# Inverse deviations of all norms by GpSimd's power, and a new hand-over between blocks, in a four-layer hybrid network

## The chip, the core and the metric

The kernel runs on one core of a Trainium2 chip. The core has a matrix engine (TensorE, PE in the profile; its weight loads are shown apart as PEld), a vector engine (VectorE, DVE), an engine for activation functions (ScalarE, ACT), a general engine (GpSimd, POOL) and an engine that in this kernel only issues transfers (SyncE, SP). Each works through its own instructions in order and waits at semaphores for the others. The metric is the device time of one launch in microseconds (us): the median of several runs. One execution is profiled, and every duration below is from it.

## What is computed

The input is four images of 128 channels and 64 x 64 pixels in float32. Four layers follow each other, each with a residual sum and a norm ahead of it:

```python
# layers 0 and 1: norms over groups of 4 channels (_gn)
x = x + L0_conv(_gn(x), ...)      # depthwise convolutions, sorting of patches, a state-space scan
x = x + L1_conv(_gn(x), ...)      # 3x3 convolution
t = _to_tokens(x)                 # 4096 tokens of 128 channels an image
t = t + L2_attn(_ln_t(t), ...)    # attention, 16 heads of 8, then a small feed-forward part
t = t + L2_ffn(_ln_t(t), ...)     # 64 experts, each picks its 8 best tokens
t = t + L3_attn(_ln_t(t), ...)    # linear attention
t = t + L3_ffn(_ln_t(t), ...)     # 64 experts again

def _ln_t(v, eps=1e-5):
    m = jnp.mean(v, axis=-1, keepdims=True)
    s = jnp.var(v, axis=-1, keepdims=True)
    return (v - m) / jnp.sqrt(s + eps)
```

Inside layer 2's attention, with t already normed:

```python
attn_out = ctx @ w_comb.T + b_comb
x1 = _ln(x + attn_out, g1, beta1)           # x is the normed input
zf = jnp.cos(x1[..., :8]) * jnp.cos(ry_theta)
h = jax.nn.relu(zf @ w1.T + b1)
return _ln(x1 + h @ w2.T + b2, g2, beta2)
```

What matters here is the factor 1/sqrt(s + 1e-5), which every norm needs once a token (or once a channel in `_gn`).

## The kernel before

Tokens or pixels lie along the free dimension, 128 channels on the partitions, and the 4096 columns of an image are worked through in 8 chunks of 512 (`NCH`, `CH`). Four stretches follow each other in time.

**Layers 0 and 1** (`layers01`, lines 270 to 1074). The first image is brought into sorted order alone (`in_order`); then `scan` runs over all four images, 8 chunks each, while the preparation of the next image, or the convolution of a finished one, runs beside it. In the scan the order of the instructions of all five engines is the written one (`tc.manual_schedule`). Small steps are put off with `later` and issued at the next `flush`, which stands between the decays (L908, ScalarE) and the scans (L912, VectorE) of every half step; GpSimd multiplies the states at L916. The groupnorm (`groupnorm_scale`) takes its root at L204 and inverts it at L200; the pixel norm takes its roots for four chunks together at L654, inverts at L659, and spreads them with transposes at L668.

**Layer 2** (`layer2_attention`). For each image b, a stage with planned order runs `prepare(b)` (norm, cosines, products, stores of the heads) beside `feed_forward(b - 1)` (what follows the attention of the image before); then `attention` of image b runs, with the written order on TensorE, VectorE and GpSimd. Outside the parts in `manual_schedule`, the framework's planner orders the instructions by the time at which it thinks them ready, and by the order of the program among the ready ones. `run` takes a step of each of its parts in turn. `feed_forward` is a chain of nine stages a chunk: `fetch` (den, num, nrm_in), `divisors`, `attended`, `first_centred`, `first_norm`, `cosines`, `hidden`, `last_centred`, `last_norm`; so there are two norms a chunk in it, and one in `prepare`. The first 1024 columns of an image (its chunks 0 and 1) get a further sum, from `around_d`: `attention` stores for each head h the sums `accs[h][:, 0]` as one [128, 256] block (L1437), and `gathered` reads them for a chunk with 16 transfers, one a head (L1583). `divisors` turns den's 2 x 16 rows to columns with a matmul against `pick`, which adds the two halves.

**The shared norm** (`layernorm_steps`, L99 to L126). TensorE subtracts the mean (`ln_xc`); ScalarE squares (L107) and copies (L109); TensorE takes the mean of the squares (`ln_var`); VectorE transposes 32 x 32 blocks (L115), so that four variances lie in columns; ScalarE takes the root (L117), VectorE inverts it (L118), TensorE spreads the four columns with transposes against the identity (L121), and VectorE multiplies (L123, or L125 with a GpSimd addition at L126). `first_centred` gives it two terms: `w_comb` times the attended sums and `center` times nrm_in.

**The experts** (`expert_ffn`, twice) **and layer 3** (`layer3_attention`, between them). `weigh` goes through 16 steps a pair of images: `centred`, `deviation` (a transpose of 64 x 512 at L1782, the root at L1784, the inverse at L1785, a transpose back at L1786) and `gates`. The second pair's steps run beside `collect` of the first. Layer 3 runs `summed(b + 1)`, with the shared norm in it (L1973), beside `answered(b)`; image 0's `summed` runs alone.

In the profile, ScalarE has besides its activations instructions named ACT_TABLE_LOAD, which stand ahead of an activation whose function needs another table than the one in place.

Of the kernel before, what the change touches and what calls it, by code (L numbers as in the profile page):

```python
# [30 lines left out]
class Common:  # L31
# [3 lines left out]
    def __init__(self, tc, pool):  # L35
# [18 lines left out]
        self.eps5 = const("eps5", [P, 1], 1e-5)  # L54
# [44 lines left out]
    def layernorm_steps(self, out, terms, work, psum, affine=None, bufs=2):  # L99
# [7 lines left out]
        nc.scalar.activation(sq, xc, AF.Square, bias=shift)  # L107
        kept = work.tile([P, CH], F32, name="ln_kept", bufs=bufs)
        nc.scalar.activation(kept, xc, AF.Identity, bias=shift)  # L109
# [6 lines left out]
        sd = work.tile([P, 4, 1], F32, name="ln_sd")  # L116
        nc.scalar.activation(sd, vt[:, :, 0:1], AF.Sqrt, bias=self.eps5)  # L117
        nc.vector.reciprocal(sd, sd)  # L118
        by_block = vp.rearrange("p (g b i) -> p b g i", b=4, i=32)
        for k in range(4):  # L120
            nc.tensor.transpose(by_block[:, k], sd[:, k].to_broadcast([P, P]), self.ident)  # L121
        if affine is None:
            nc.vector.tensor_tensor(out, kept, vp, ALU.mult)  # L123
        else:
            nc.vector.scalar_tensor_tensor(kept, kept, g, vp, ALU.mult, ALU.mult)  # L125
            nc.gpsimd.tensor_scalar(out, kept, b, None, ALU.add)  # L126

# [35 lines left out]
    def groupnorm_scale(self, xb, xp, small, psum):  # L163
# [33 lines left out]
        sd = small.tile([P, 1], F32, name="gn_sd")  # L197

        def offset():
            nc.vector.reciprocal(rs, sd)  # L200
            nc.vector.scalar_tensor_tensor(off, gm, -1.0, rs, ALU.mult, ALU.mult)

        def deviation():
            nc.scalar.activation(sd, vp, AF.Sqrt, bias=self.eps5)  # L204
            self.later(offset)
# [64 lines left out]
def layers01(K, xd, dpool, w, w1):  # L270
# [9 lines left out]
    with ExitStack() as ctx:  # L280
# [145 lines left out]
        def in_order(b, made, work, psum):  # L426
# [208 lines left out]
            spreads = small.tile([P, NCH, 4], F32, name="spreads")  # L635
# [3 lines left out]
            def varied(c):  # L639
# [12 lines left out]
                def root():  # L652
                    at = spreads[:, c - 3 : c + 1]
                    nc.scalar.activation(at.unsqueeze(3), kept["vt"][:, :, :, 0:1], AF.Sqrt, bias=K.eps5)  # L654
                    later(inverted)

                def inverted():
                    at = spreads[:, c - 3 : c + 1]
                    nc.vector.reciprocal(at, at)  # L659
# [4 lines left out]
            def scaled_by_root(n):  # L664
                bp = K.bank(psum, [P, CH], "pos_rs")
                by_block = bp.rearrange("p (g b i) -> p b g i", b=4, i=32)
                for k in range(4):
                    nc.tensor.transpose(by_block[:, k], spreads[:, n, k : k + 1].to_broadcast([P, P]), K.ident)  # L668
# [436 lines left out]
def layer2_attention(K, xd, dpool, w):  # L1105
# [6 lines left out]
    with ExitStack() as ctx:  # L1112
# [48 lines left out]
        pick = cst.tile([2 * NH, NH], F32, name="pick")  # L1161
        nc.vector.tensor_tensor(pick, K.ident[0 : 2 * NH, 0:NH], K.ident[0 : 2 * NH, NH : 2 * NH], ALU.add)
# [22 lines left out]
        around_d = dpool.tile([NH, P, L // NJ // 4], F32, name="around_d")  # L1185
# [135 lines left out]
        def attention(qt, first, dsum, big, two, work, pssc, psctx, psacc):  # L1321
# [83 lines left out]
            def turn():  # L1405
# [28 lines left out]
                if i == 0:  # L1434


                    nc.sync.dma_start(out=around_d[h], in_=accs[h][:, 0].rearrange("p t r -> p (t r)"))  # L1437
# [121 lines left out]
        def feed_forward(b, dsum, work, psum):  # L1559
# [17 lines left out]
            def gathered(c):  # L1577
# [4 lines left out]
                for h in range(NH):  # L1582
                    nc.sync.dma_start(  # L1583
                        out=part[HD * h : HD * h + HD],
                        in_=around_d[h, :, c * P : (c + 1) * P].rearrange("(n d) f -> d n f", d=HD),
                    )
                    if h % 4 == 3:
                        yield
                yield
# [8 lines left out]
            def firsts():  # L1598
                for c in order[NCH - CHB :]:
                    yield from gathered(c)  # L1600

            def divisors(c):
                num, den, at = loads[c]
                tp = psum.tile([P, 4, NH], F32, name="den_t", tag="mm")
                for j in range(4):
                    mm(tp[:, j, :], den[:, j * P : (j + 1) * P], pick)
                rd = work.tile([P, 4, NH], F32, name="rd")
                nc.vector.tensor_tensor(rd, tp, dsum[:, 4 * c : 4 * c + 4], ALU.add)
# [13 lines left out]
            def first_centred(c):  # L1622
# [3 lines left out]
                    x1, [(w_comb, num[:, 0]), (K.center, nrm)], work, psum, (b_comb, g1, beta1), bufs=3  # L1626
# [47 lines left out]
        for b in range(NB + 1):  # L1674
            with (
# [3 lines left out]
                with (  # L1679
# [3 lines left out]
                    parts = list(feed_forward(b - 1, past, work, psum)) if b > 0 else []  # L1683
                    if b < NB:
                        part, qt, first = prepare(b, big, two, work, psum)
                        parts.append(part)
                    run(*parts)
# [15 lines left out]
def expert_ffn(K, xs, w, tag):  # L1703
# [10 lines left out]
    with ExitStack() as ctx:  # L1714
# [47 lines left out]
        def weigh(pr):  # L1762
# [3 lines left out]
            sqs = {}  # L1766
# [367 lines left out]
```

## Time and profile before

| What | us |
|---|---|
| median of 3 runs (9885.13 to 9886.97) | 9885.43 |
| the profiled execution, its own time | 9881.09 |
| its span, first to last instruction | 9879.3 |
| busy: PE / DVE / ACT / POOL | 8736.1 / 7220.5 / 7410.6 / 4802.8 |
| mean granted TensorE clock | 0.92 |

The stretches in time, read from the windows of the profile (us from the start of the span):

| Stretch | from | to | length |
|---|---|---|---|
| first image brought in order | 0 | 190 | 190 |
| scan, with the work beside it | 190 | 2645 | 2455 |
| last convolution | 2645 | 2745 | 100 |
| first `prepare`, alone | 2745 | 2880 | 135 |
| four attentions | | | 1291, 1291, 1293, 1290 |
| three stages with `feed_forward` and `prepare` | 4171 | 4371 | 200 each |
| last `feed_forward`, alone | 8627 | 8765 | 138 |
| experts of layer 2 | 8765 | 9130 | 365 |
| layer 3 | 9130 | 9520 | 390 |
| experts of layer 3 | 9520 | 9880 | 360 |

A line of the list of groups reads: line of the kernel, engine, operation, written tile <- read tiles, shapes, count | busy time in all, mean ns of one | idle time of the engine just before, and what ended it. A line of the timeline gives start, length, engine, line, operation and, in brackets, the idle time before it and its releaser. A line of the windows gives the stretch, its length, the busy time of PE, PEld, DVE, ACT and POOL with their instructions, the granted clock, the share of the transfer engines and GB/s.

### The profile page before, as it was taken

Reading aid. Unit: us, or ns where it says so; the run is one execution under the profiler, and the core shown is the slowest. Engines: PE = TensorE matmul, PEld = TensorE weight load, DVE = VectorE, ACT = ScalarE, POOL = GpSimd, SP = SyncE. Lnnn points to the kernel's source line nnn. Section 1 sums busy time; section 2 is a strip of 40 time slices with the busy share of each in tenths; the row PEclk is TensorE's granted clock in tenths of the full one; section 3 lists DMA queues with packets and bytes.
Section 4 is the critical chain, followed back from the end, with each engine's and each line's share of the span. In section 5 each row is a group of like instructions: output and inputs, shape, how many; then the busy total and the mean of one; then the engine's idle time right before and its main releaser. Section 6 shows DMA issues by size and latency. Waiting matters only on the chain.

```text
span 9879.3 us, 187787 instructions
## 1 busy us (share of the span) xinstructions
PE 8736.1 (88%) x74074; PEld 3348.6 (34%) x74074; DVE 7220.5 (73%) x7877; ACT 7410.6 (75%) x10669; POOL 4802.8 (49%) x3175
## 2 busy tenths in 40 slices
PE   5888888888869999989999989999989999967776
PEld 2222222244523333333333333333333333333433
DVE  2889897988658888758888758888758888743463
ACT  3766767654359999879999879999879999841531
POOL 1677676765435555455555455555455555420000
PEclk8887878889979999989999989999989999988997
DMA  4524435223121221231111131211131211124004
GB/s 116 124 69 118 97 83 125 67 76 88 46 70 40 40 40 41 48 94 39 40 39 41 46 97 39 40 40 39 44 101 39 39 40 39 40 93 121 1 18 154
DMA packets 575731, 635.31 MB, mean 64 GB/s; under 512 B 113080, under 2 KB 369152, under 8 KB 573824
## 3 DMA queue, kind: packets, MB, share of 16 engines
q1 hardware_dynamic: 574848, 623.30, 25.6%
q8 instruction: 584, 9.57, 0.4%
q14 instruction: 299, 2.45, 0.1%
HBM read 446.84 MB, written 109.07 MB: 56 GB/s over the span
## 4 chain that ended last, share of the span: by engine, by line
PE 69%; DVE 10%; POOL 6%; ACT 5%; DMA 4%; issue 3%; SPq 2%; DVEq 0%; POOLq 0%; ACTq 0%
PE ctx_ps L91 27%; PE acc_ps L91 13%; PE score L91 11%; PE conv L91 4%; DVE hs L912 3%; POOL hs L916 3%; PE ln_xc L91 2%; PE y_ps L91 2%; DVE hs L901 2%; PE xc_ps L91 1%; DMA w<-in_L_ffn_weight 1%; PE ln_var L91 1%; PE b_ps L91 1%; PE hid_ps L91 1%; PE kv L91 1%
## 5 line engine op out<-in xcount | busy, mean ns | idle before, releaser
L1535 ACT ACTIVATE ex<-score 128x1024 f32<-128x1024 f32 x5120 | 4925.4, 1036 | 218.5 <-PE score L91 125.7
L91 PE MATMUL ctx_ps<-ex,qt 128*32 128x512 f32 x20480 | 2733.9, 606 | 19.9 <-DVE ctx L1469 19.9
L1484 POOL TENSOR_TENSOR folded<-ex 128x1024 f32<-128x1024 f32 x512 | 1224.2, 2391 | 2101.5 <-ACT ex L1535 1836.6
L1541 DVE STREAM_TRANSPOSE turned<-ex 128x1024 f32<-128x1024 f32 x1536 | 1885.8, 1228 | 329.1 <-ACT ex L1535 328.7
L1517 DVE STREAM_TRANSPOSE turned<-ex 128x1024 f32<-128x1024 f32 x1532 | 1842.4, 1203 | 0.0
L91 PE MATMUL acc_ps<-turned,turned_v 128*32 128x256 f32 x24576 | 1769.5, 379 | 3.1 <-POOL qt L1229 2.3
L912 DVE TENSOR_TENSOR_SCAN hs<-decay,carry,hs 128x512 f32<-128x512 f32 x1024 | 1245.7, 1266 | 193.6 <-ACT decay L908 180.1
L91 PE MATMUL score<-queries,keys 32*128 32x512 f32 x10240 | 1335.3, 497 | 44.0 <-POOL queries L1219 37.9
L91 PEld LDWEIGHTS acc_ps<-turned,turned_v 128*32 128x32 f32 x24576 | 800.9, 110 | 1476.5 <-issue 1323.8
L916 POOL TENSOR_TENSOR hs<-hs,c_sb 128x1024 f32<-128x1024 f32 x512 | 1207.3, 2358 | 81.4 <-DMA c_sb<-c_d 40.3
L908 ACT ACTIVATE decay<-dt,a_neg 128x512 f32<-128x512 f32 x1024 | 693.0, 689 | 662.5 <-DVE hs L912 653.3
L91 PEld LDWEIGHTS score<-queries,keys 32*128 32x128 f32 x10240 | 512.6, 182 | 1139.2 <-ACT ex L1535 780.9
L1347 POOL TENSOR_TENSOR turned_v<-v,quarter 128x1024 f32<-128x1024 f32 x256 | 612.4, 2393 | 265.7 <-PE acc_ps L91 225.0
L91 PE MATMUL y_ps<-hs,pair 128*64 128x512 f32 x2048 | 661.5, 773 | 33.6 <-POOL hs L916 33.6
L1485 POOL TENSOR_TENSOR quarters<-folded 128x512 f32<-128x512 f32 x512 | 657.7, 1285 | 40.2
L91 PEld LDWEIGHTS ctx_ps<-ex,qt 128*32 128x32 f32 x20480 | 406.4, 108 | 654.7 <-issue 598.7
L901 DVE TENSOR_TENSOR hs<-dtx,b_ps 128x2048 f32<-128x2048 f32 x256 | 580.1, 2266 | 55.9 <-PE b_ps L91 31.6
L91 PE MATMUL b_ps<-dbc,state 32*64 32x512 f32 x1024 | 343.2, 752 | 233.4 <-DVE hs L901 233.2
L1535 ACT ACTIVATION_READ_ACCUMULATOR ex<-score 128x1 f32 x2048 | 435.9, 213 | 0.0
L915 POOL COPY carry<-hs 128x2 f32<-128x2 f32 x512 | 98.1, 192 | 673.4 <-DVE hs L912 652.0
L1469 DVE COPY ctx<-ctx_ps 128x512 f32<-128x512 f32 x256 | 176.9, 691 | 329.3 <-PE ctx_ps L91 327.0
L1526 DVE TENSOR_REDUCE dacc<-quarters 128x2 f32<-128x512 f32 x508 | 327.1, 644 | 0.0
(371 smaller groups left out, 9016.1 us busy)
## 6 DMA issues: line engine op xcount, KB each, us to landing
c_sb<-c_d SPq DMA_DIRECT2D x512, 128.0 KB
queries<-head_d SPq DMA_DIRECT2D x1024, 64.0 KB
keys<-head_d SPq DMA_DIRECT2D x1024, 64.0 KB
under<-image_d SPq DMA_DIRECT2D x192, 264.0 KB
dt<-dt SPq DMA_DIRECT2D x128, 256.0 KB
dtx<-dtx SPq DMA_DIRECT2D x128, 256.0 KB
v<-value_d SPq DMA_DIRECT2D x1024, 32.0 KB
w<-in_L_ffn_weight SPq DMA_DIRECT2D x32, 1024.0 KB
```

The costliest lines, as they stand in the source:

```text
L91: self.nc.tensor.matmul(out, lhsT, rhs, start=start, stop=stop)
L901: nc.vector.tensor_tensor(hs, dtx2, bb.unsqueeze(1).to_broadcast([P, NQ, CH]), ALU.mult)
L908: nc.scalar.activation(ex, dt2[:, q, :], AF.Exp, scale=a_neg[:, q, g : g + 1])
L912: nc.vector.tensor_tensor_scan(hs[:, q, :], decays[q - 2 * i], hs[:, q, :], carry[:, g, q : q + 1], ALU.mult, ALU.add)
L916: nc.gpsimd.tensor_tensor(hs[:, two, :], hs[:, two, :], cs.unsqueeze(1).to_broadcast([P, 2, CH]), ALU.mult)
L1347: nc.gpsimd.tensor_tensor(t, v.unsqueeze(2).to_broadcast([P, 4 * BT, 4, HD]), quarter.unsqueeze(1).to_broadcast([P, 4 * BT, 4, HD]), ALU.mult,
L1484: nc.gpsimd.tensor_tensor(hs, exs[:, :, 0], exs[:, :, 1], ALU.add)
L1485: nc.gpsimd.tensor_tensor(qs, hs[:, :, 0 : CH // 2], hs[:, :, CH // 2 :], ALU.add)
L1517: nc.vector.transpose(*upright)
L1526: nc.vector.tensor_reduce(at, qs, AX.X, ALU.add)
L1535: nc.scalar.activation(ex, sps[p], AF.Exp, scale=scale, accum_out=sums[:, t : t + 1] if summed else None)
L1541: nc.vector.transpose(*upright)
```

## The change

Roots: ScalarE's Sqrt and VectorE's reciprocal give way to an addition of 1e-5 on VectorE and a power of -0.5 on GpSimd, everywhere.

```diff
-        sd = work.tile([P, 4, 1], F32, name="ln_sd")
-        nc.scalar.activation(sd, vt[:, :, 0:1], AF.Sqrt, bias=self.eps5)
-        nc.vector.reciprocal(sd, sd)
+        sd = work.tile([P, 4], F32, name="ln_sd")
+        self.inverse_root(sd, vt[:, :, 0])()
...
+    def inverse_root(self, out, src):
+        p, n = out.shape
+        self.nc.vector.tensor_scalar(out, src, 1e-5, None, ALU.add)
+        return lambda: self.nc.gpsimd.tensor_tensor(out, out, self.minus_half[0:p, 0:n], ALU.pow)
...
         def offset():
-            nc.vector.reciprocal(rs, sd)
             nc.vector.scalar_tensor_tensor(off, gm, -1.0, rs, ALU.mult, ALU.mult)
         def deviation():
-            nc.scalar.activation(sd, vp, AF.Sqrt, bias=self.eps5)
+            self.inverse_root(rs, vp)()
             self.later(offset)
```

In the pixel norm the addition is issued at one flush and the power, with `roots[0]`, at the next (`root`, `inverted`). In the expert gates the transpose back becomes a stage of its own, so that it comes one step after the power:

```diff
-                sd = work.tile([P, CH // 32, 1], F32, name="ln_sd")
-                nc.scalar.activation(sd[half], vt[half, :, 0:1], AF.Sqrt, bias=K.eps5[half])
-                nc.vector.reciprocal(sd[half], sd[half])
+                sd = sds[n] = work.tile([P, CH // 32], F32, name="ln_sd")
+                nc.vector.tensor_scalar(sd[half], vt[half, :, 0], 1e-5, None, ALU.add)
+                nc.gpsimd.tensor_tensor(sd[half], sd[half], K.minus_half[half], ALU.pow)
+
+            def spreaded(n):
...
-            return in_turn(2 * NCH, centred, deviation, gates)
+            return in_turn(2 * NCH, centred, deviation, spreaded, gates)
```

The first block's sums: the layout of `around_d` is turned, each head but the last stores 16 pieces of 8 rows, the last head stores one block of its own, and a chunk is read with two transfers.

```diff
+                    sums = accs[h][:, 0].rearrange("p t r -> p (t r)")
+                    if h + 1 < NH:
+                        for k in range(16):
+                            r = slice(HD * k, HD * k + HD)
+                            nc.sync.dma_start(out=around_d[k, HD * h : HD * h + HD], in_=sums[r])
+                    else:
+                        nc.sync.dma_start(out=around_last_d, in_=sums)
...
-                for h in range(NH):
-                    nc.sync.dma_start(
-                        out=part[HD * h : HD * h + HD],
-                        in_=around_d[h, :, c * P : (c + 1) * P].rearrange("(n d) f -> d n f", d=HD),
-                    )
-                    if h % 4 == 3:
-                        yield
-                yield
+                cols = slice(c * P, (c + 1) * P)
+                r = HD * (NH - 1)
+                nc.sync.dma_start(out=part[0:r], in_=around_d[:, 0:r, cols].rearrange("n q f -> q n f"))
+                nc.sync.dma_start(out=part[r:], in_=around_last_d[:, cols].rearrange("(n d) f -> d n f", d=HD))
+                yield from [None] * 4
...
             def firsts():
+                yield from [None] * 12
```

The divisors and the first inner norm: den is turned with transposes, and its halves are added on VectorE; nrm_in is added on VectorE (argument `more`) and no longer goes through `center`, and ScalarE's copy falls away there.

```diff
-                    mm(tp[:, j, :], den[:, j * P : (j + 1) * P], pick)
+                    nc.tensor.transpose(tp[:, j, :], den[:, j * P : (j + 1) * P], K.ident[0 : 2 * NH, 0 : 2 * NH])
                 rd = work.tile([P, 4, NH], F32, name="rd")
-                nc.vector.tensor_tensor(rd, tp, dsum[:, 4 * c : 4 * c + 4], ALU.add)
+                nc.vector.tensor_reduce(rd, tp.rearrange("p j (z h) -> p j h z", z=2), AX.X, ALU.add)
+                nc.vector.tensor_tensor(rd, rd, dsum[:, 4 * c : 4 * c + 4], ALU.add)
...
-                    x1, [(w_comb, num[:, 0]), (K.center, nrm)], work, psum, (b_comb, g1, beta1), bufs=3
+                    x1, [(w_comb, num[:, 0])], work, psum, (b_comb, g1, beta1), bufs=3, more=nrm
...
+        if more is not None:
+            nc.vector.scalar_tensor_tensor(kept, xc, shift, more, ALU.add, ALU.add)
+            nc.scalar.activation(sq, kept, AF.Square)
```

The hand-over: `prepare`'s steps stand ahead of `feed_forward`'s in each turn.

```diff
-                    parts = list(feed_forward(b - 1, past, work, psum)) if b > 0 else []
+                    parts = []
                     if b < NB:
                         part, qt, first = prepare(b, big, two, work, psum)
                         parts.append(part)
+                    if b > 0:
+                        parts.extend(feed_forward(b - 1, past, work, psum))
```

## The prediction

> **What bounds the kernel now.** I read the page's busy row and its table loads first, then the stages by windows, then the order of time inside the stages that the change touches. ScalarE's table loads in the list of groups (count, busy time, mean ns):
>
> ```profile
> L117 ACT ACT_TABLE_LOAD x93 | 119.3, 1283 | 3.8 <-DVE ln_vt L115 2.2
> ...
> L241 ACT ACT_TABLE_LOAD x58 | 74.4, 1283 | 1.0
> ...
> L2023 ACT ACT_TABLE_LOAD x24 | 30.8, 1283 | 0.4
> ...
> L204 ACT ACT_TABLE_LOAD x8 | 10.3, 1283 | 0.1
> L1992 ACT ACT_TABLE_LOAD x8 | 10.3, 1283 | 0.1
> ```
>
> L117 and L204 (with L654, 7 loads, and L1784, 3) are square roots of norms; L241 (Sin) and L2023/L1992 (Exp) mostly load back what a square root drove out. No Square, Identity, Relu or Copy line has a load in these stages, so without the roots one table stays for a whole stage. The stages, by windows (length; then busy time of PE, weight loads, DVE, ACT, POOL; granted clock):
>
> ```profile
> 190.00:2645.00 2455.00, 2042.21 (x7253) 735.36 (x7252) 2085.76 (x1734) 1536.85 (x2056) 1667.62 (x1263) 0.84 0.37 92
> 2745.00:2880.00 135.00, 44.17 (x178) 22.68 (x178) 58.71 (x144) 50.88 (x74) 41.60 (x69) 0.56 0.37 98
> 2880.00:4171.00 1291.00, 1283.04 (x14592) 453.03 (x14592) 1036.39 (x1055) 1237.23 (x1792) 679.23 (x353) 1.00 0.19 38
> 4171.00:4371.00 200.00, 145.43 (x666) 73.73 (x666) 95.33 (x219) 127.84 (x193) 96.28 (x112) 0.80 0.46 128
> 9220.00:9520.00 300.00, 237.64 (x976) 127.20 (x970) 188.87 (x386) 166.35 (x255) 0.58 (x2) 0.99 0.02 6
> ```
>
> The four attention blocks (third row, 1291 us each) are full of TensorE work, 1283 of 1291; the change leaves that work alone. The scan (first row) is paced by VectorE. The rest, a first preparation (135 us), three handovers from block to block (200 each), a last feed-forward (138) and layer 3 (390), has no full engine: there latency decides. In layer 3's steady loop, one chunk takes 10.24 us:
>
> ```profile
> 9240.32 1.28 ACT L117 ACT_TABLE_LOAD   x1
> 9240.70 0.31 DVE L115 STREAM_TRANSPOSE ln_vt<-ln_var 128x128 f32<-128x128 f32 x1
> ...
> 9241.41 1.02 PE L91 MATMUL o_ps<-vn,wo 128*128 128x512 f32 x2
> 9241.62 0.30 ACT L117 ACTIVATE ln_sd<-ln_vt,eps 128x4 f32<-128x4 f32 x1
> ...
> 9242.47 0.75 DVE L2047 SCALAR_TENSOR_TENSOR x<-o_ps,bo,x 128x512 f32<-128x512 f32 x1 [1.46 <-PE o_ps L91]
> 9242.51 1.28 ACT L2023 ACT_TABLE_LOAD   x1
> 9243.14 0.17 DVE L118 RECIPROCAL ln_sd<-ln_sd 128x4 f32<-128x4 f32 x1
> ...
> 9243.36 0.65 PE L121 MATMUL ln_var<-ident,ln_sd 128*128 128x128 f32 x4 [0.93 <-DVE ln_sd L118]
> ```
>
> The root comes so late that the reciprocal (L118) falls behind L2047 on VectorE, and TensorE stands 0.93 us before L121, although its o_ps work ended at 9242.43.
>
> **The price of the power.** No row raises to a power. Its cheapest neighbours on GpSimd are the 128x2 copy at L915 (0.19 us) and the 128x64 product at L1269 (0.31). From above I bound it by GpSimd's dearest elementwise pass, 2.39 us for 128x1024 (L1484): a power of 4 columns would then cost as much as 256 products a column. It is nearest to the small rows but does more per element: I take 0.5 us for 4 columns and 1.0 for 16, ends 0.19 and 2.4. The addition of 1e-5 on VectorE stands in for the reciprocal (0.17 and 0.25 us) and costs no more. A root today, where it needs its load, takes 1.28 + 0.30 + 0.17 = 1.75 us.
>
> The Trainium skill's "GPSIMD Engine Reference", section 3.1, speaks against the edit: elementwise work there costs about twice VectorE's time, and a freshly loaded kernel's first call pays about 6 us. The first half agrees with this trace (1.27 us at L1667 against 0.69 at L123, both 128x512); no row here shows the second. By the page the sum below would be some 6 us higher.
>
> **Part by part.** (a) Layer 3, 24 steady chunks: L115 ends at 9241.01, the addition at about 9241.1, the power at 9241.6, before o_ps ends (9242.43). L121 then starts 0.93 earlier, of which I count 0.85: -20 us. At 2.4 us a power ends at 9243.5, 0.2 after today's reciprocal: +5.
>
> (b) Its first 8 chunks, alone, 11.41 us each: the Exp load (9142.71 to 9144.00) holds up ln_sq behind it, 1.2 us; then ln_vt ends at 9146.07, and the power at 9146.7 stands against the reciprocal at 9147.52, 0.9. Seven periods x 2.1 = -15; at the dear end -1.
>
> (c) The first preparation, 10.95 us a chunk: ln_vt is ready at 2791.21, but the root's load waits for Abs on ScalarE and L118 ends at 2793.36. With the power at 2791.8 and Sin without its load, 2 us x 7 = -14; dear end 0.
>
> (d) The last feed-forward: TensorE is nearly full there (110 of 138). Removed per chunk: the centring product of nrm_in (1.02 us, 8699.09) and half of den_t's eight passes (1.06 us, 8701.02; four transposes are left), 1.55 x 8 = -12; its starting gathers hold den's second load at SP from 8630.43 to 8637.18, -6. Sum -18.
>
> (e) Three handovers. TensorE's waits there: "PE ln_var L121 <- DVE ln_sd L118: 26.6, 13" and "PE ln_xc L91 <- DMA x_in<-xd: 8.0, 1". Of the 26.6 I give back half (13), since the power now queues behind GpSimd passes of 1.3 to 2.4 us. x_in, today issued at 4175.18 behind eight other transfers and landing in 7.74, goes first and may land in the 3.97 of the first preparation (2751.77): 3.6 + 3.8, so -7. Of the 12.4 us of removed matmul work (8 x 1.55) some 5 lies bare, TensorE being busy 145 of 200. Together -25 each, -75; dear end -10 each.
>
> (f) The scan and the start: 16 roots in groupnorms and pixel norms, 12 of them in the scan. Six powers of groupnorms in the scan queue behind products of 2.35 us on GpSimd, and VectorE's gn_off waits: the flush for gn_off comes one slot later (289.37), and the power could end at 287.9 or, behind the other product, at 290.2: 0 to 1 us each, +3. Given back: 12 loads and their returns on ScalarE, busy 63% there, whose lateness costs VectorE 180 us in all; 30 us of 1537 would be 3.5. Zero, with the start -4 (three roots there, little beside them: 1.28 + 0.3 less each).
>
> (g) The expert gates: transposes of root n move one stage later. Two steps take 5.69 us (8821.94 to 8827.63), TensorE busy 42 of 50; the power of 16 columns must fit in one step, 2.84, and one more stage of depth eats what the shorter wait gives: 0.
>
> (h) The sums: fifteen heads x 16 stores of 8 rows in place of one. A store of the same form (num_d, L1474) takes SP 0.30 us from issue to issue, so 16 x 0.30 - 0.34 = 4.5 us a head. SP's waits in a block (343 on ctx, 154 on turned_v, 98 on acc) sum to over half of its 1291 us, so this hides; behind it stand loads of v for GpSimd, two steps ahead. Bare, it would cost 4.5 x 15 x 4 = 270. The fetch shrinks from 16 issues to 2 a chunk and is counted in (d) and (e).
>
> The Trainium skill's "DMA: Bandwidth & Descriptors", rules for kernel authors, says that transfers under 64 KB pay mostly overhead and should be joined. That speaks against (h)'s 8 KB stores; the SP rows show the 16 KB num_d stores hidden behind waits. By its fixed 2 us each, one after another, a block would have 240 x 2 = 480 us more of transfers.
>
> VectorE takes over the sum with nrm (0.75 us, by L125) and a reduction of den (0.25, by L1608), eight times a handover: 95 + 8 = 103 of some 175, hidden.
>
> Sum: -20 - 15 - 14 - 18 - 75 - 4 = -146 against the profiled run's 9881.1 (span 9879.3), giving 9735; the median of the runs, 9885.4, stands 4.3 above it, so 9740. The dear ends give +5 - 1 + 0 - 18 - 30 = -44, so 9841. Cheap ends: in each handover all of 26.6 + 8 + 12.4 (141 for three), 1.3 a chunk in (a) (31), (b) 15, 2.6 a chunk in (c) (18), 24 in (d), 4 in (f): -233, so 9650.
>
> **The rivals.** *GpSimd becomes the queue in the handovers.* It is busy 96 of 200, 24 powers make it 108, and it serves in order: a power behind L126 (1.56) and L1667 (1.27), themselves waiting for VectorE, arrives as late as the root did. For it: "POOL x L126 <- DVE ln_kept L125: 11.6" shows it standing at its head. Against: the root stands behind four hid activations (2.4 us) in the same way. Then only x_in and the matmuls count there, -12 each, and (c) and (d) halve: -36 - 20 - 15 - 7 - 9 - 4 = -91, so 9795.
>
> *The power is dear per element, and the expert gates become its queue.* If it costs 0.6 us a column (2.4 for 4, 9.6 for 16), 32 steps in the bare gates of 2.84 us and 32 beside the collection (67 us for 16, 4.2) grow to 9.6: 216 + 173 = 389 us, against -44 of the rest: 10230. It decides from about 0.33 us a column, where 5.2 us a step costs 75 + 32 = 107 and the rest gives about as much. Against: even 0.33 a column is 140 times L1484's 2.3 ns.
>
> *The loads lie beside other work*, and the handovers end on the load of the next block's keys (SP issues 16 from 4334.07, 11 us). Then (a) to (c) shrink to nothing measurable: 9885.
>
> *Everything shrinks and the clock follows* (0.56 and 0.80 granted in the stages that shorten): the cheap ends and some 25 us of faster matmuls, 9625.
>
> **How the numbers follow.** Forecast 0.52 (own range 9690 to 9790), GpSimd queue 0.27, dear power 0.12, hidden 0.05, larger gain 0.04. The predicted time is the forecast's, 9740. The range 9640 to 9890 takes in both ends of the unknown costs and leaves out the dear power, the larger gain and part of the hidden case, under 2 in 10. A difference under 0.2% (20 us) can't be told from none. Faster: 0.52 + 0.27 + 0.04 = 0.83; same 0.05; slower 0.12.
>
> **What would show it.** Right: L117, L204, L654 and L1784 gone, some 190 loads fewer in all (190 x 1.283 = 244 us of ScalarE); layer 3's period near 9.4 us; handovers near 175; attention blocks still 1291; small powers on GpSimd of 0.3 to 1.3 us. Wrong: powers of several us with TensorE waiting for GpSimd at L121; VectorE waiting for GpSimd in the scan; attention blocks longer through SP.

## The result, and the profile after

The changed kernel takes 10024.7 us (median of 4 runs, 10022.6 to 10034.1) against 9885.3 (9883.1 to 9887.0) for the kernel before, run beside it: a ratio of 1.0141, 95% interval 1.0126 to 1.0156. It is slower by 139 us, where 145 us less were forecast. The profiled execution has a span of 10032.3 against 9879.3, 153 more.

First the list of groups after (line, engine, operation, tiles, count | busy, mean ns | idle before and what ended it), the rows of the new power and of those who wait for it:

```profile
L1796 POOL TENSOR_TENSOR ln_sd<-ln_sd,minus_half 64x16 f32<-64x16 f32 x64 | 185.3, 2895 | 269.6 <-DVE ln_sd L1795 269.6
...
L135 POOL TENSOR_TENSOR ln_sd<-ln_sd,minus_half 128x4 f32<-128x4 f32 x128 | 136.7, 1070 | 433.1 <-DVE ln_sd L134 250.8 <-PE q_ps L91 173.1 <-PE kv_sum L91 8.7
...
L124 PE MATMUL ln_var<-ident,ln_sd 128*128 128x128 f32 x512 | 101.1, 331 | 195.9 <-POOL ln_sd L135 193.6
...
L1800 DVE STREAM_TRANSPOSE rs<-ln_sd 64x512 f32<-64x512 f32 x64 | 45.2, 706 | 195.7 <-POOL ln_sd L1796 195.7
...
L135 POOL TENSOR_TENSOR spreads<-spreads,minus_half 128x16 f32<-128x16 f32 x8 | 23.4, 2930 | 2.5 <-DVE spreads L134 2.5
```

The waits of the first handover (engine, tile and line <- releaser: us in total, times, longest), the three rows at its head:

```profile
PEld ln_var L124 <- POOL ln_sd L135: 63.6, 24, 7.4
PE ln_var L124 <- POOL ln_sd L135: 50.5, 22, 7.1
POOL ln_sd L135 <- DVE ln_sd L134: 32.5, 13, 6.1
```

A power takes 1.07 us for 4 columns and 2.9 for 16, whether on 64 or 128 partitions. VectorE stands 196 us ahead of L1800 and TensorE 196 ahead of L124 (115 at L121 before), both for a power; 50.5 of the latter in this one handover, where 26.6 went to the reciprocal before.

The windows of the changed kernel, for the stretches that the prediction showed (length; busy time of PE, weight loads, DVE, ACT, POOL; granted clock, transfer share, GB/s): scan, first preparation, first attention, first handover, steady layer 3.

```profile
195.00:2678.00 2483.00, 2046.44 (x7268) 739.30 (x7266) 2086.22 (x1736) 1504.76 (x2022) 1688.90 (x1275) 0.84 0.36 91
2780.00:2912.00 132.00, 44.88 (x180) 23.10 (x180) 56.26 (x144) 30.91 (x52) 48.43 (x77) 0.53 0.41 101
2912.00:4201.00 1289.00, 1281.58 (x14592) 452.00 (x14592) 1036.21 (x1056) 1237.58 (x1792) 678.34 (x352) 1.00 0.21 38
4201.00:4402.00 201.00, 125.89 (x608) 59.48 (x608) 113.50 (x234) 77.96 (x130) 119.79 (x133) 0.81 0.49 124
9323.00:9612.00 289.00, 243.51 (x976) 131.01 (x974) 190.68 (x385) 98.91 (x183) 24.75 (x26) 0.97 0.02 7
```

In the handover (fourth row) TensorE has 20 us less to do than before (125.9 against 145.4) and ScalarE 50 less, and yet it lasts longer: only GpSimd (119.8 against 96.3) and VectorE rose. From marks in both traces (first and last instructions of each stage) comes where the 153 us arose:

| stage | before | after | forecast (term) | measured |
|---|---|---|---|---|
| start and scan, to the last groupnorm | 2676.2 | 2710.2 | -4 (f) | +34 |
| first preparation, from the first product with x_in to the first score | 125.0 | 121.7 | -14 (c) | -3 |
| four attentions | 1289 to 1291 | 1290 each | 0 (h) | -3 |
| three handovers, from dsum to the next score | 195.7, 195.7, 193.5 | 201.3, 201.8, 201.7 | -75 (e) | +20 |
| last feed-forward, to the first step of the gates | 163.8 | 164.6 | -18 (d) | +1 |
| expert gates, four times 16 steps | 216 in all | 354 in all | 0 (g) | +138 |
| layer 3, first to last step of its norm | 327.7 | 299.9 | -35 (a, b) | -28 |
| the last experts' end | | | | -6 |

### The profile page after: what moved, and what is told of

Its sections match the earlier page's. It is cut to its first block, busy times and chain, and to the rows that moved or that the text cites. A ratio compares the mean times of both kernels' runs of the same rounds, so it can differ in the third digit from the quotient of the medians.

```text
span 10032.3 us, 188091 instructions
## 1 busy us (share of the span) xinstructions
PE 8710.5 (87%) x73882; PEld 3311.1 (33%) x73882; DVE 7271.9 (72%) x7940; ACT 7067.3 (70%) x10219; POOL 5156.5 (51%) x3383
## 5 line engine op out<-in xcount | busy, mean ns | idle before, releaser
L135 POOL TENSOR_TENSOR ln_sd<-ln_sd,minus_half 128x4 f32<-128x4 f32 x128 | 136.7, 1070 | 433.1 <-DVE ln_sd L134 250.8
```

## The experiments

Ratios are to the kernel before on the same chip, whose median lay between 9886 and 9895. Theory P at first: the power is long and stands where the next instruction waits for it. Rival S: the stores, the new fetch and the new order cost the time.

**Four parts put back alone.** The gates' roots:

```diff
-                nc.vector.tensor_scalar(sd[half], vt[half, :, 0], 1e-5, None, ALU.add)
-                nc.gpsimd.tensor_tensor(sd[half], sd[half], K.minus_half[half], ALU.pow)
+                nc.scalar.activation(sd[half].unsqueeze(2), vt[half, :, 0:1], AF.Sqrt, bias=K.eps5[half])
+                nc.vector.reciprocal(sd[half], sd[half])
```

> The changed kernel with only the expert gates' norms back to square root (ScalarE) and reciprocal (VectorE), in their old stage. Theory P (the power is long, 2.9 us for 16 columns, and stands in a serial chain): the four weighings lose what the changed kernel added there, 35 us each: about 10025 - 138 = 9887, a step of the gates back at 2.84 us. Rival S (the stores, the fetch, the new order and the sum with nrm cost the time, the power only rides along): at most 20 us less than 10025.

Measured: 9907 us, 1.0014 (1.0004 to 1.0023), some 125 us less than the changed kernel. Nine tenths of the loss lie in the gates.

The root of 4 columns in `layernorm_steps` put back (Sqrt at `sd`, then the reciprocal):

> The changed kernel with only the norms of 4 columns (layernorm_steps: first preparation, handovers, feed-forwards, layer 3) back to square root and reciprocal. Theory P: each handover falls from 202 us to below the 195.7 of before (170 to 190, since the cheaper fetch and the four instead of eight den passes are still there), 3 x 12 to 30 less, while layer 3 loses its gain of 27 and the first preparation 3: 9965 to 10020. Rival S: handovers stay at about 202 and layer 3 gives its gain back: about 10055.

Measured: 1.0137 (1.0120 to 1.0154), no difference from the changed kernel. The time lies above P's range. The handovers fall to 186.4, 185.7 and 187.0 and the last feed-forward to 150.8, as P had it, but layer 3 gives back more than it had gained (336 us from the first to the last step of its norm, against 300 in the changed kernel and 328 in the kernel before). So in the 4-column norms loss and gain cancel, and the power costs a handover 15 us.

The groupnorms' and the pixel norm's roots put back:

> The changed kernel with only the norms outside layernorm_steps and the gates (groupnorms and the pixel norm in front of the scan) back to square root and reciprocal. Theory P: the start gives back 8 us and the scan 10 us for each of three images (the images' starts lay 8.3, 17.8, 26.3 and 37.1 us later than before), so about 10025 - 34 = 9991. Rival S': the scan is paced by VectorE, and the delay comes from the delayed order of the work, not from the power: no more than 10 us less.

Measured: 1.0105 (1.0090 to 1.0120), 36 us less; the last groupnorm comes at 2677.8. As P had it.

All roots put back, nothing left but the stores, the fetch, den, the sum with nrm and the order:

> The changed kernel with every square root and reciprocal back and no power left: only the stores by eights, the fetch by two transfers, den by transposes, the sum with nrm on VectorE and the order with the preparation first remain. Theory P: these parts gain by themselves, handovers of 170 to 190 us in place of 195.7 and a last feed-forward some 15 us shorter: 9790 to 9870. Rival S: they cost: handovers of 200 or more, 9900 or more.

Measured: 9858 us, 0.9964 (0.9951 to 0.9977). Handovers 187.5, 185.2, 185.6, the last feed-forward 153.1: rival S falls. The rest of the change gains 35 us, the powers lose 175.

One thing in this run is not the work of the parts that are left: layer 3 takes 343 us from the first to the last step of its norm, 16 more than in the kernel before, though its steps are the same. The windows of its first eight chunks and of the rest, in the kernel before, the changed kernel and this run:

```profile
9136.00:9221.00 85.00, 57.29 (x241) 38.90 (x242) 22.16 (x52) 42.59 (x66) 0.00 (x0) 0.75 0.00 0
9221.00:9464.00 243.00, 197.57 (x876) 110.96 (x874) 148.17 (x310) 152.67 (x233) 0.00 (x0) 1.00 0.00 1
```

```profile
9252.00:9324.00 72.00, 48.23 (x250) 32.24 (x242) 22.99 (x56) 20.27 (x42) 8.09 (x8) 0.88 0.00 0
9324.00:9552.00 228.00, 198.36 (x870) 113.09 (x870) 148.71 (x306) 85.55 (x161) 23.16 (x23) 0.98 0.00 1
```

```profile
9100.00:9194.00 94.00, 65.64 (x242) 42.68 (x242) 22.41 (x51) 42.32 (x64) 0.00 (x0) 0.66 0.00 0
9194.00:9443.00 249.00, 203.01 (x875) 115.46 (x874) 149.59 (x307) 152.00 (x232) 0.00 (x0) 0.96 0.00 1
```

In the first eight chunks the granted clock was 0.66 here, 0.75 before and 0.88 with the power. All six runs with the root back in layer 3 show 336 to 343 us; why is open.

**Why 2.9 us cost 2.15 a step in the gates.** An empty stage between the power and the spreading should let VectorE go on:

```diff
-            return in_turn(2 * NCH, centred, deviation, spreaded, gates)
+            return in_turn(2 * NCH, centred, deviation, lambda n: None, spreaded, gates)
```

> The changed kernel with one empty stage put between the power of the expert gates and the spreading of its result, so that VectorE goes on with the next step before it waits for GpSimd. Theory P1 (what costs is the wait in a closed ring: transpose 0.71, add 0.17, power 2.9, spreading 0.70, about 5.0 us a step): the step falls to what GpSimd needs alone, 2.9 to 3.1 us, 64 x 1.9 to 2.1 less: about 9895 to 9905. Rival P2 (GpSimd or its hand-overs slow down the whole loop whatever the depth): 4.5 us a step or more, 9990 or above.

Measured: 1.0129 (1.0112 to 1.0146), nothing gained. The timeline of this run (start, length, instruction, in brackets the idle time before it and its releaser) shows why:

```profile
8849.57 0.70 DVE L1800 STREAM_TRANSPOSE rs<-ln_sd 64x512 f32<-64x512 f32 x1 [3.04 <-POOL ln_sd L1796]
...
8850.31 0.72 DVE L1793 STREAM_TRANSPOSE ln_vt<-ln_var 64x512 f32<-64x512 f32 x1
...
8851.06 0.17 DVE L1795 TENSOR_SCALAR ln_sd<-ln_vt 64x16 f32<-64x16 f32 x1
...
8851.38 2.90 POOL L1796 TENSOR_TENSOR ln_sd<-ln_sd,minus_half 64x16 f32<-64x16 f32 x1 [1.84 <-DVE ln_sd L1795]
...
8854.31 0.71 DVE L1800 STREAM_TRANSPOSE rs<-ln_sd 64x512 f32<-64x512 f32 x1 [3.08 <-POOL ln_sd L1796]
```

The planner moved the spreading (L1800) straight behind the addition (L1795) all the same. In the changed kernel it stands there by the program's own order: `in_turn` issues the stages of a turn from the last to the first, so `spreaded` of a step comes ahead of the next step's `deviation`, and on VectorE only a product for the gates can lie between the addition and the spreading. VectorE serves in order: transpose 0.72, addition 0.17, then 3.08 idle for the power, spreading 0.71, and only then the next step's transpose, which feeds the next power. GpSimd idles 1.84 in turn. It is a closed ring of 4.7 us; in the changed kernel every second step has a product for the gates in it and takes 5.3, 5.0 on average.

The next run takes one power of 128x16 and one spreading for two steps:

> The changed kernel with one power of 128x16 for each two steps of the expert gates in place of two of 64x16, and one spreading for both, a stage later. Theory P1: 64 partitions cost as much as 128, so GpSimd needs 1.46 us a step and falls behind TensorE's 2.45: a step takes 2.45 to 2.85 us, no longer than the 2.84 of the square root: 9860 to 9890, at or below the 9907 that the gates with the square root gave. Rival P3 (128 partitions cost twice what 64 cost, 5.8 us): a step of 2.9 to 3.1, about 9900.

Measured: 1.0030 (1.0019 to 1.0040); the first sixteen transposes of ln_vt take 47.2 us against 74.9 in the changed kernel. The power of 128x16 takes 2.90: P3 falls. But a step, 3.1, is still over P1's range: there are half as many rings, and none is opened, for VectorE still idles 3.08 us ahead of each spreading.

So VectorE's order was written out, on top of the empty stage:

```diff
+        with tc.manual_schedule(engines={mybir.EngineType.DVE}):
             run(weigh(0))
             choose(0)
             run(weigh(1), collect(0))
```

> As the run with an empty stage, and besides VectorE's order in the weighings is the program's own instead of the planner's (which had put the spreading straight behind the addition again, so that the empty stage changed nothing). Theory P1 (the closed ring through VectorE's order is what costs): a step falls from 5.0 to what GpSimd needs, 2.9 to 3.2 us, 64 x 1.8 to 2.1 less: 9890 to 9910. Rival P2: 4.5 us a step or more, 9990 or above.

Measured: 9909 us, 1.0021 (1.0011 to 1.0030). VectorE's timeline in the same part:

```profile
8852.57 0.67 DVE L1793 STREAM_TRANSPOSE ln_vt<-ln_var 64x512 f32<-64x512 f32 x1
8853.27 0.17 DVE L1795 TENSOR_SCALAR ln_sd<-ln_vt 64x16 f32<-64x16 f32 x1
8853.97 0.71 DVE L1800 STREAM_TRANSPOSE rs<-ln_sd 64x512 f32<-64x512 f32 x1 [0.53 <-POOL ln_sd L1796]
8855.11 0.72 DVE L1793 STREAM_TRANSPOSE ln_vt<-ln_var 64x512 f32<-64x512 f32 x1 [0.44 <-PE ln_var L91]
```

The addition at 8853.27 belongs to a later step than the spreading at 8853.97, which waits 0.53 in place of 3.08. Power follows power on GpSimd (eight in 23.7 us), and a step takes 3.03 (45.4 for fifteen). The four weighings take 236 us in all, against 354 in the changed kernel: 118 of the 138 us are gone with the same powers. The empty stage alone had given nothing, so it was VectorE's order that closed the ring; the 2.9 us were only its condition. The written order takes in VectorE's part of `choose` and `collect` too, and it was not run without the empty stage.

**The handovers.** Theory Q: GpSimd is the queue there. Rival L: the power's own time in the chain of a norm. The beta addition moved off GpSimd:

```diff
-            nc.gpsimd.tensor_scalar(out, kept, b, None, ALU.add)
+            nc.scalar.activation(out, kept, AF.Identity, bias=b)
```

> The changed kernel with the last addition of the affine norms (beta) moved from GpSimd (1.57 us each, 16 a handover) to ScalarE (0.68). Theory Q (in the handovers GpSimd is the queue: the powers stand with its other passes, 120 of 202 us busy against 97 with the square root): handovers fall from 202 to 182 to 190, the last feed-forward from 165 to about 150: 9950 to 9975. Rival L (what counts is the time of the power itself between VectorE's addition and TensorE's transposes): handovers 197 or more, 10005 to 10025.

And the other way round, roots back and a power that nothing reads:

```diff
+        idle = work.tile([P, 4], F32, name="ln_idle")
+        nc.gpsimd.tensor_tensor(idle, sd, self.minus_half[:, 0:4], ALU.pow)
```

> The changed kernel with the square root and the reciprocal back in layernorm_steps, and besides a power of 4 columns on GpSimd for each of them whose result nothing reads. Theory Q: GpSimd's time alone costs: handovers rise from 186 (the run with the square root back) to 196 or more and the last feed-forward from 151 to 158 or more: 10060 to 10090. Rival L: nobody waits for it, so handovers stay at 184 to 190: 10020 to 10040.

Measured: without the additions handovers of 192.9, 192.6, 194.2 and the last feed-forward 160.2, 1.0105 (1.0090 to 1.0120). With the idle power 196.1, 194.9, 195.0, but the last feed-forward stays at 150.0; 1.0160 (1.0145 to 1.0176). The handovers lie between the ranges of the two theories (with the idle power at the edge of Q's), and both runs say that GpSimd's time alone makes some 9 of the 15 us. (The addition also became shorter, 0.72 us on ScalarE against 1.6 on GpSimd; but in handovers without powers, below, moving it brings nothing.) In the last feed-forward, without a preparation beside it, an idle power costs nothing. By exclusion the 14 us (150.8 to 164.6) are put down to the power's place in the chain, rival L.

GpSimd's timeline at the end of the second handover, with TensorE's first score of the next block, changed kernel, then the run with all roots back:

```profile
5879.39 1.04 POOL L135 TENSOR_TENSOR ln_sd<-ln_sd,minus_half 128x4 f32<-128x4 f32 x1 [2.35 <-DVE ln_sd L134]
5886.57 1.01 POOL L135 TENSOR_TENSOR ln_sd<-ln_sd,minus_half 128x4 f32<-128x4 f32 x1 [6.15 <-DVE ln_sd L134]
5887.54 1.89 POOL L1223 CAST keys<-keys 128x2048 fp32r<-128x2048 f32 x1
...
5892.27 1.89 POOL L1223 CAST queries<-queries 128x2048 fp32r<-128x2048 f32 x1
...
5894.22 1.47 PE L91 MATMUL score<-queries,keys 32*128 32x512 f32 x6 [5.93 <-POOL queries L1223]
```

```profile
5818.15 1.56 POOL L131 TENSOR_SCALAR blk<-ln_kept,beta 128x512 f32<-128x512 f32 x1
5825.53 1.56 POOL L131 TENSOR_SCALAR blk<-ln_kept,beta 128x512 f32<-128x512 f32 x1 [5.82 <-DVE ln_kept L130]
5827.05 1.89 POOL L1232 CAST keys<-keys 128x2048 fp32r<-128x2048 f32 x1
...
5837.89 1.20 PE L92 MATMUL score<-queries,keys 32*128 32x512 f32 x6 [0.95 <-issue]
```

The rounding of the next block's keys (CAST) comes 40 us after SP began to load them (5847.4) in the changed kernel, behind the power of the last chunk; without powers 23 us (from 5804.0). TensorE then stands 5.93 us ahead of the first score for the rounding of the queries, in all three handovers, and 0.95 without powers (7.03 with the idle power). Two runs were to tell whether this place costs. Roundings on ScalarE:

```diff
-                        rounded(first[0])
+                        nc.scalar.copy(first[0], first[0].bitcast(F32))
```

> The changed kernel with the roundings of the next block's first keys and queries moved from GpSimd to ScalarE. Theory H (in GpSimd's queue the rounding of the keys stands behind the power of the last feed-forward chunk, 40 us after its load began): the rounding comes 24 to 30 us after the loads begin, handovers fall from 202 to 186 to 193: 9985 to 10005. Rival L (the power's own length delays the last chunks, and the block has to wait for these anyway): handovers 198 or more, 10015 to 10030.

Measured: handovers 197.0, 196.7, 197.2, 1.0122 (1.0107 to 1.0137), between the two. The rounding still came 38 us after the loads began, now behind the last chunk's squares on ScalarE, but TensorE waits only some 1 us for it (0.96, 1.22, 0.96). The other makes the last two powers read their exponent from a tile written after the roundings:

```diff
+                    K.exponents.append(two.tile([P, 4], F32, name="exponent"))
+                    nc.gpsimd.tensor_scalar(K.exponents[-1], t[:, 0:4].bitcast(F32), 0.0, -0.5, ALU.mult, ALU.add)
```

> The changed kernel with a dependence added: the last two powers of a handover take their exponent from a small tile that GpSimd writes from the rounded keys and queries, so that both roundings stand ahead of these powers in GpSimd's queue. Theory H (the place in the queue costs): the rounding of the keys comes about 24 us after the loads begin in place of 40, and handovers fall from 202 to 188 to 195: 9990 to 10010. Rival L (the last chunks' own norms hold the block, whatever comes first): handovers 198 or more, 10012 or more.

Measured: handovers 195.0, 199.4, 194.4, 1.0120 (1.0105 to 1.0135), at the upper end of H's range, the second handover outside it; the rounding of the keys comes 29.6 us after the loads began, and the first score, 0.91 us after TensorE's last work, no longer waits for it. So in both runs the wait for GpSimd's rounding, 5 us of the 15, is gone; that overlaps with the 9 of GpSimd's time. What remains is taken to lie in the last chunks' norms, which TensorE's order has ahead of the first score. How the 15 divide further was not settled.

**The rest of the change, part by part,** each on the run without any power (handovers 186 us). The sum with nrm undone:

```diff
-                    x1, [(w_comb, num[:, 0])], work, psum, (b_comb, g1, beta1), bufs=3, more=nrm
+                    x1, [(w_comb, num[:, 0]), (K.center, nrm)], work, psum, (b_comb, g1, beta1), bufs=3
```

> The run without any power (all square roots and reciprocals back, 0.9964 of before), and besides nrm goes again through the centring product into ln_xc and is not added on VectorE. Theory M (the removed product is what made the handovers shorter, 8 x 1 us of matmul and no wait behind it): handovers go from 186 to 190 to 196 and the last feed-forward from 153 to 158 or more: 0.9978 to 1.0000 of before. Rival N (the sum puts VectorE between the product and the square, which takes the gain back): handovers 183 to 188, 0.994 to 0.997.

Measured: handovers 190.6, 194.2, 189.8; 0.9984 (0.9974 to 0.9993). The removed product is worth 5 us a handover. In the last feed-forward it is worth nothing (152.0 us with it, 153.1 without), where theory M had 158 or more. The order undone (`feed_forward` first in `parts`):

> The run without any power, and besides the feed-forward stands ahead of the preparation again. Theory O (the preparation first makes x_in land earlier and the handover shorter, as the step of x_in in the prediction has it): handovers 190 to 196, 0.9978 to 0.9995 of before. Rival N2 (the order is not what counts, the fewer fetches and matmuls are): handovers 183 to 188, 0.9955 to 0.997.

Measured: handovers 175.8, 177.5, 177.1; 0.9939 (0.9924 to 0.9953). Neither theory: the new order costs 9 us a handover. SP's timeline of the second handover, first with the preparation first (it began at 5652.7), then with the feed-forward first (5639.3):

```profile
5803.66 0.34 SPq L1686 DMA_DIRECT2D xd<-x  x1
5804.05 0.68 SPq L1224 DMA_DIRECT2D queries<-head_d  x1
```

```profile
5782.05 0.34 SPq L1686 DMA_DIRECT2D xd<-x  x1
5782.44 0.68 SPq L1224 DMA_DIRECT2D queries<-head_d  x1
```

In SP's queue the loads of the next queries and keys stand behind the feed-forward's third store of x, here as in the kernel before and the changed one. That store comes 151 us into the handover when the preparation goes first and 142.8 when it does not, and the block starts 34 us behind it in both. What the preparation wins early is lost, because its own last loads wait for the other part. That the store is what holds them is read from the order and the times; it was not tried apart.

The old stores and fetch on top of that (`around_d` by heads, sixteen transfers a chunk, no delay):

> The run without any power and with the feed-forward first, and besides the sums are again stored by one transfer a head and fetched by sixteen a chunk. What is left of the change is den by transposes and the sum with nrm. Theory F (fetch: the first chunks of the feed-forward start earlier, SP is free for x_in): handovers rise from 177 to 185 to 192, the last feed-forward from 152 to 158 or more: 0.9965 to 0.999 of before. Rival M2 (the removed matmuls did it all): handovers 176 to 180, 0.9935 to 0.995.

Measured: handovers 192.0, 191.4, 190.8, the last feed-forward 160.2, 0.9996 (0.9986 to 1.0005), a little above F's range. The new stores, the fetch by two transfers and its delay by twelve turns are together worth 15 us a handover and 8.5 in the last feed-forward. Attention takes 1290 us either way: the small stores stay hidden.

**The scan.** The pixel norm's root alone put back:

> The changed kernel with the square root and reciprocal back in the pixel norms alone (16 columns, two in each image); the groupnorms keep their power of 1 column. Theory: the transposes of the roots stand in TensorE's hand-written order one slot behind a power of 2.9 us and waited 27.5 us for it in seven places; with the root back nearly all of the scan's 36 us return: 9988 to 10000, 1.0100 to 1.0112 of before. Rival: the groupnorms' powers behind products of 2.4 us cost it: 10010 or more, 1.0125 or more.

Measured: 1.0116 (1.0101 to 1.0131), some 25 of the 36 us, a little short of the range. The changed kernel's answer for the tile of the roots, part "who waited for it" (us, times):

```profile
  PEld pos_rs L673: 27.5, 7
  ACT ln_rs L677: 20.6, 6
  PE pos_rs L673: 20.5, 7
```

Seven times the weight loads stood some 4 us behind a power of 2.9 in an order that was written for a reciprocal of 0.24; before, TensorE's two rows came to 2.8 us in all. The remaining 11 us would be the groupnorms'; but the last groupnorm of runs with the same scan code came anywhere from 2704.5 to 2721.5, so that share is uncertain.

**Putting together what gains.** The power only in the first preparation and in layer 3:

> The run without any power, and besides the power back in the norms of 4 columns of the first preparation and of layer 3 alone. The theory that the power gains where GpSimd is idle and TensorE waits for the root: 36 to 45 us less than without any power, 0.9918 to 0.9930 of before. Rival: the layer-3 gain hung on the tables of the whole kernel: 0.995 or more.

Measured: 9803 us, 0.9911 (0.9897 to 0.9926), a little below the theory's range. Layer 3 is shorter by 44 us than with the root in the same surroundings (28 against the kernel before, where its first chunks had the clock of 0.75), the first preparation by 10. With the feed-forward first and paired powers in the gates:

> The gathered sums, den by transposes and the sum with nrm as in the change, the feed-forward first, the power only in the first preparation, in layer 3 and, as one power of 128x16 for two steps and with VectorE's order written out, in the expert gates; square roots everywhere else. If the parts add up: 0.9911 - 0.0025 for the order, and a step of the gates of 2.45 to 2.6 us in place of 2.84, 64 x 0.25 to 0.4, 0.0016 to 0.0026 less: 0.986 to 0.9875 of before. If the gates are bound by something else than the root: 0.9885 or more.

Measured: 9777 us, 0.9884 (0.9867 to 0.9900). The order adds up; the gates do not: a step takes 2.86 (2.87 with the root), so something else bounds them, which was not looked for. With roots in the gates and beta on ScalarE instead:

> The gathered sums, den by transposes and the sum with nrm as in the change, the feed-forward first, the power only in the first preparation and in layer 3, square roots elsewhere and in the expert gates, and the beta addition of the affine norms on ScalarE. By the runs so far 0.9884 without the last part. If GpSimd's time counts in the handovers without the power too: 5 to 9 us a handover less, 0.986 to 0.987. If ScalarE, which has the roots and their tables there, becomes the later one: 0.9885 to 0.991.

Measured: 9773 us, 0.9877 (0.9860 to 0.9893), between the two ranges; handovers about 175 against 174. Where there is no power, moving the beta addition brings nothing in the handovers; the last feed-forward is 4.7 us shorter (146.8 against 151.5), and three of the attentions are 2 to 3 us longer. Both kernels beat the kernel before by some 110 to 120 us, and can't be told apart.

## Why the prediction was wrong, by its steps

- **The price of the power** was put at 0.5 us for 4 columns and 1.0 for 16. The rows give 1.07 and 2.9: some 0.4 us and 0.156 a column. The 4 columns lay within the bounds (0.19 to 2.4); the 16 got the estimate nearest to the cheap rows, and came out above the upper end as well. The Trainium skill's "GPSIMD Engine Reference" has the first call of some 6 us, for a freshly loaded kernel, in section 2.1 (not in 3.1, which has the twofold time); here the groupnorm's powers took 0.55 to 0.57 us from the first on, so no run shows it.
- **(g), the step that failed most** (138 of 153): "the power of 16 columns must fit in one step, 2.84, and one more stage of depth eats what the shorter wait gives: 0". It compared GpSimd's time with the step and so took the added stage for depth. On the chip the stage gave none: on VectorE the spreading stood straight behind the addition, and the step became a sum over two engines, 5.0 us. The rival of the dear power had the right place, but its point of decision (0.33 us a column, 5.2 us a step) counted the power alone; the ring decided it at 2.9.
- **(e), three handovers, -75 forecast, +20 measured.** The ledger from the runs, for one: 195.0 before; den and the sum with nrm -3.6; the stores and the fetch -14.6; the preparation first +9.3; the power +15.5; 201.6 after. "Of the 26.6 I give back half (13)" had the wrong sign: TensorE waits 50.5 us for powers there. "x_in goes first" was right in its mechanism (TensorE's wait for x_in fell from 8.3 to 4.2 us in the second handover), and worth nothing: the new order costs 9 us a handover, by the reading above because SP's queue ties the end of the preparation to the feed-forward. The fetch with its stores, which (e) did not count on its own, was the largest gain: joined transfers, as the Trainium skill's "DMA: Bandwidth & Descriptors", rules for kernel authors, wants them.
- **(d) -18, +1.** Without power the last feed-forward is 11 to 13 us shorter than before (153.1 and 150.8), but not by the terms of (d): the fetch, put at 6, gave 8.5, and the removed product, 8 of the 12 us of matmul work, gave nothing. The power in the chain took the gain back, 14 us. Its delay, an addition that VectorE reaches late and a power of 1.04, was costed nowhere in (d).
- **(f) -4, +34.** The prediction looked at the six groupnorms in the scan. The pixel norm's power of 16 columns, which makes most of it, had no term: its root was counted among the loads given back.
- **(a), (b) -35, -28: right in the mechanism, a little large in size.** The first eight chunks gained 14 us, where (b) has 15, the rest 14, where (a) has 20. (b) took 11.41 us for each chunk, but they took 9.6 to 11.4; and the granted clock rose there from 0.75 to 0.88, which (b) did not count, so that its size is partly luck. "Layer 3's period near 9.4 us" came out: the additions at L134 come 9.44 us apart (9344.47, 9353.91, 9363.34). In the changed kernel's timeline (lines of other work left out) the power ends at 9345.80 and L124 follows at once, right behind o_ps, where TensorE had stood 0.93 us before:

```profile
9344.47 0.17 DVE L134 TENSOR_SCALAR ln_sd<-ln_vt 128x4 f32<-128x4 f32 x1
...
9344.71 1.02 PE L91 MATMUL o_ps<-vn,wo 128*128 128x512 f32 x2
...
9344.79 1.01 POOL L135 TENSOR_TENSOR ln_sd<-ln_sd,minus_half 128x4 f32<-128x4 f32 x1 [8.43 <-PE q_ps L91]
...
9345.85 0.65 PE L124 MATMUL ln_var<-ident,ln_sd 128*128 128x128 f32 x4
```

- **(c) -14, -3** here, -10 in the run with the power there and in layer 3 alone; the mechanism holds, the size varies.
- **(h) 0: right.** Sixteen stores a head leave attention at 1290 us. The 480 us of transfers are an estimate from the same page's fixed 2 us, which its section "Anatomy of one DMA — SWDGE (gpsimd) path" gives for transfers issued from GpSimd, and these are issued by SP; no run here shows them.

ScalarE did become lighter by 343 us (7410.6 to 7067.3); 269 of them are table loads (518 before, 308 after), where 244 were forecast. The stretches got shorter by it only in layer 3 and the first preparation.

## What to carry to other kernels

An operation moved to another engine is priced by the ring it closes: follow what its reader's engine has to do next, in the order in which that engine will do it. A stage added for depth is worth nothing until the trace shows other work between producer and reader; where a planner orders the instructions, look at its order, or write it. An idle engine is a gain only where it is idle: the same power gained 28 us in layer 3 and lost 15 in every handover.

## What was not expected of the hardware

The power's time goes with the columns, not with the partitions: 0.56 us for 128x1, 1.07 for 128x4, 2.90 for 64x16 and 2.90 for 128x16. And replacing sixteen transfers of 8 rows a chunk by two, with the stores and the delay that go with it, shortened a handover by 15 us, in which the transfer engines had been busy for less than half of the time (0.46).
